# A four-direction selective scan: y kept in its direction's order, empty turns around DMAs, small operations moved from GpSimd to VectorE

## The chip, the cores and the metric

The kernel runs on one core of one Trainium2 chip. The metric is the device time of one execution in microseconds, the median of several runs. The engines are TensorE (PE, with PEld for its weight loads), VectorE (DVE), ScalarE (ACT), GpSimd (POOL) and SyncE (SP), which here issues all DMAs. Each takes its instructions in the order in which the program gives them, and waits at the first whose inputs are not ready.

## The reference, cut to what matters

The program is a sequence of four layers on x of shape (8, 64, 64, 64); the change touches the first one alone. There each image is normalised, projected to 128 channels of L = 4096 places, convolved (3 x 3, each channel by itself), scanned in four directions, normalised again, gated and projected back:

```python
xc = silu(_dwconv3(xc, conv_w, conv_b))
x_flat = xc.reshape(B, DI, L)                                   # row by row
x_t = jnp.transpose(xc, (0, 1, 3, 2)).reshape(B, DI, L)         # column by column
xs = jnp.concatenate([x_hwwh, jnp.flip(x_hwwh, axis=-1)], axis=1)
def step(h, inp):
    u_t, dt_t, B_t, C_t = inp
    h = h * jnp.exp(dt_t[..., None] * A) + dt_t[..., None] * B_t[:, :, None, :] * u_t[..., None]
    return (h, jnp.einsum('bkcn,bkn->bkc', h, C_t))
y = out_y[:, 0] + inv[:, 0] + wh + invwh                        # all put back in row order
y = _ln(y, outnorm_g, outnorm_b, LN_EPS) * jax.nn.silu(z)
return jnp.einsum('bhwd,cd->bhwc', y, outproj_w) + outproj_b
```

So a state of N = 16 numbers for each of 128 channels runs along L four times, and the four results are summed into y, place by place.

## The kernel before, in words

The 128 channels are the partitions. An image is 16 *steps*: four directions of four chunks of CH = 1024 places. A step has 16 *turns*, one for each n of the state. `steps` gives the order of directions: 0, 2, 1, 3 (rows forward, rows backward, columns forward, columns backward) and in the last image 1, 3, 0, 2, so that it ends in rows.

One turn (the loop at `for n in range(N)` and `unit`, L757 to 775):

- `z` is B_n of the chunk, spread over the partitions: by two matmuls from the bf16 pieces `bs` into PSUM (L737), or, for n in `BY_POOL` = (0, 3, 6, 8), by a product on GpSimd (L727) that ScalarE copies to PSUM (L734).
- ScalarE computes `a` = exp(dt A) (L719).
- VectorE multiplies `z` by dt u (L764; not for n in `BY_POOL`), then runs the scan `h` over 1024 places (L768).
- GpSimd multiplies `ct`, which a DMA has spread from DRAM (L715, 512 KB a turn, five buffers), by `h` (L773).
- TensorE sums `ct` into the chunk's PSUM tile `yps` (L810), two or three turns later (`sum_up`).

At turn 3 `begin_sum` opens the sum of the step: in an image's first direction from u (`skipd`), later from what y holds so far (L801). At turn 2 `empty` has had ScalarE copy the step before it out of PSUM into y (L783). The last chunk of a direction is the first of its reverse, so there the PSUM tile is kept and neither is needed. y lies in row order; for the column directions `ordered` reads and writes it with a stride of 64 elements.

Around that, `Background` holds a queue of *items*, each a pair (make, use): make's matmuls are issued in one turn, use's work on other engines in the next; `bg.later` puts a DMA another turn later. `(None, None)`, called `none`, is an empty turn. Turns in `idle` take an item only if it has no make. The items are the input norm, gates and convolutions of the next image, the projections of the next step (put first), and the output norm, gating and projection of the image before. `inverse_root` makes the two norms' chain: variances go to DRAM (`put`), come back spread over partitions (`fetch`), ScalarE takes the root, VectorE inverts, and the result goes to DRAM and comes back in rows (`back`), for a matmul that spreads it (`rps`, L393 and L445). In the last image the output norm is done two blocks at a time as they become ready, two items a turn.

The bf16 `pieces` of B (L667 to 700): one DMA brings `bw`, ScalarE rounds it to the first piece, GpSimd subtracts it (L681), ScalarE rounds the rest to the second (L684), GpSimd subtracts again for the third (L687), and DMAs store the three. `hooks` lays these, the step size's `soft` parts and `step_input` on turns 6 to 13 of each step. The gating product `z` times y is `multiply` (L566), on GpSimd, called from the norm's `apply` after the product of the next block.

Of the kernel before, what the change touches and what calls it, by code (L numbers as in the profile page):

```python
# [18 lines left out]
NB = 8  # L19
C = 64  # L20
S = 64
# [144 lines left out]
class Background:  # L166
# [7 lines left out]
    def __init__(self):  # L174
        self.queue, self.last, self.late = deque(), None, []
        self.groups, self.open, self.done = deque(), deque(), {}
        self.first = self.credit = 0
        self.item = False

    def add(self, items, first=False):  # L180
# [41 lines left out]
    def finish(self, b, count):  # L222

        while self.done.get(b, NBK) < count:
            self.credit = 1
            self.before(slots=NBK)
            self.after()

    def drain(self):
# [5 lines left out]
def scan_layer(cm, x_in, w, xh):  # L235

    tc, nc = cm.tc, cm.nc
    with ExitStack() as ctx:
# [90 lines left out]
        def inverse_root(nb):  # L329

            var = dr.tile([L], F32, name="vard", tag="vard")[: nb * BK]
            rs = dr.tile([L], F32, name="rsd", tag="rsd")[: nb * BK]
            sm = {}

            def put(ps, n, at):
                t = work.tile([NBK, BK], F32, name="vrow", tag="rstd", bufs=1)
                nc.scalar.copy(t[:n], ps[:n])
                bg.later(lambda: nc.sync.dma_start(
                    var[at * BK : (at + n) * BK].rearrange("(o n) -> o n", o=n), t[:n]
                ))  # L340
# [12 lines left out]

            def back(_):
                sm["r"] = work.tile([NBK, BK], F32, name="rstd", tag="rstd", bufs=1)[:nb]
                nc.sync.dma_start(sm["r"], rs.rearrange("(j f) -> j f", j=nb))

            chain = [none, (None, fetch), none, (None, root), (None, invert), none, (None, back), none]
            return put, chain, sm

        def norm_x(xn, pairs, project_in):

            put, chain, sm = inverse_root(2 * len(pairs))
            i0, sq = pairs[0], {}

            def centre(i):
                def make():
                    ps = bank("cps")
                    nc.tensor.matmul(ps, ln1_cen, xn[:, i, :], start=True, stop=True)
                    return ps  # L370

                def use(ps):
                    nc.scalar.copy(xn[:, i, :], ps)
# [12 lines left out]

            def apply(i):
                r = 2 * (i - i0)

                def make():  # L390
                    ps = bank("rps")
                    rows = ln1_row[: 2 * len(pairs), r : r + 2, :].rearrange("k e c -> k (e c)")
                    nc.tensor.matmul(ps, rows, sm["r"], start=True, stop=True)  # L393
                    return ps

                def use(ps):
                    x = xn[:, i, :]
                    nc.vector.tensor_tensor(x, x, ps, ALU.mult)
                    nc.scalar.activation(x, x, AF.Identity, bias=ln1_b, scale=ln1_g)

                return make, use

            out = [centre(i) for i in pairs[:2]] + [none] * (2 - len(pairs[:2]))
            for i in pairs:
                out.append(variance(i))
                if i + 2 in pairs:
                    out.append(centre(i + 2))
            out += chain
            out += [apply(i) for i in pairs[:2]] + [none] * (2 - len(pairs[:2]))
            for i in pairs:  # L410
                out += [project_in(2 * i), project_in(2 * i + 1)]
                if i + 2 in pairs:
                    out.insert(-1, apply(i + 2))
            return out

        def norm_y(y, blocks, load, multiply, project_out):
# [38 lines left out]
                return make, use  # L455

            out = [(None, lambda _: [square(j) for j in blocks[:2]]), none]
            out += [variance(j) for j in blocks] + chain
            out.insert(-2, (None, lambda _: [load(j) for j in blocks[:3]]))
            out += [apply(j) for j in blocks[:2]]  # L460
            end = (None, lambda _: multiply(blocks[-1]))
            if nb == 2:
# [1 line left out]
            for j in blocks:  # L464
                if j + 2 in blocks:
                    out.append(apply(j + 2))
                    if j + 2 == blocks[-1]:
                        out.append(end)
                out.append(project_out(j))
            return out  # L470


# [2 lines left out]
        def before(b):  # L475
# [70 lines left out]

            items = [[(None, load(j)) for j in range(NBK)]]
            for pairs in FIRST if b == 0 else (range(NBK // 2),):
                items.append(norm_x(xn, pairs, project_in))
            return u, zd, items, [gate(j) for j in range(NBK)], [convolve(j) for j in range(NBK)]  # L550

        def after(b, y, zd, blocks=range(NBK)):
# [10 lines left out]

            def multiply(j):
                z = gated[j][1]
                nc.gpsimd.tensor_tensor(z, z, y[:, bass.ts(j, BK)], ALU.mult)  # L566

            def project_out(j):
                def make():
# [97 lines left out]
        def pieces(ctl, low):  # L667
# [10 lines left out]

            def subtract():
                low["r"] = work.tile([128, 2, 128], F32, name="br", tag="br", bufs=1)  # L680
                nc.gpsimd.tensor_tensor(low["r"], low["b"], low["p"][:, 0], ALU.subtract)  # L681

            def second():
                nc.scalar.copy(low["p"][:, 1], low["r"])  # L684

            def third():
                nc.gpsimd.tensor_tensor(low["p"][:, 2], low["r"], low["p"][:, 1], ALU.subtract)  # L687

            def store():
                low["bsd"] = dr.tile([2, 3 * N, CH], BF16, name="bsd", tag="bsd", bufs=8)  # L690
# [85 lines left out]

        full = []

        def empty():

            if full:
                ctl = full.pop()
                nc.scalar.copy(  # L783
                    ordered(ctl["y"], ctl["k"], ctl["c"]),
                    ctl["ps"].rearrange("p (a b) -> p a b", b=S),
                )

        kept = []

        def begin_sum():  # L790
# [4 lines left out]
                ctl["ps"] = kept.pop()  # L795
                return
            ctl["ps"] = psy.tile([DI, CH], F32, name="yps", tag="yps")
            wt, src = (skipd, ctl["u"]) if ctl["new_y"] else (ctl["mat"], ctl["y"])
            so, half = ordered(src, ctl["k"], ctl["c"]), BK // S
            for i in range(CH // BK):  # L800
                nc.tensor.matmul(  # L801
                    ctl["ps"][:, bass.ts(i, BK)].rearrange("p (a b) -> p a b", b=S),
# [28 lines left out]
        def prepare(b, s):  # L831

            if b not in images:
                return None
            u, zd, y = images[b]
            k, c, i = steps(b)[s]
            bg.finish(b, 2 * c + 2 if s < NCH and k == 0 else NBK)
            low = lows.setdefault((b, k % 2, c), {}) if k < 2 else lows.pop((b, k % 2, c))
            dt, ut, e, items, soft = project(u, k, c, low)
            if b == 0 and s < NCH:  # L840
# [1 line left out]
            bg.add(items, first=True)  # L842
            new = work.tile([DI, N], F32, name="state", tag="state", bufs=3)
            ctl = dict(
                k=k, c=c, u=u, y=y, dt=dt, bc=low["bc"][k // 2], ut=ut, dus=e, soft=soft, new=new, state=None,
                first=(i == 0), new_y=(s < NCH), turns=(s % (2 * NCH) == NCH - 1),
                mat=lno_cen if s >= 3 * NCH - 1 else cm.ident,
            )
# [6 lines left out]

        def start(b):
            u, zd, items, gates, convs = before(b)
            y = io.tile([DI, L], F32, name="y", tag="y")
            images[b] = (u, zd, y)
            bg.add(items[0] + items[1])  # L860
            if b == 0:
                bg.add(convs[0] + convs[1])
# [9 lines left out]
        with tc.manual_schedule():  # L872
# [15 lines left out]
            for b in range(NB):  # L888
                for s in range(4 * NCH):
# [5 lines left out]
                    else:  # L895
                        nxt = prepare(b + 1, 0)
                    bg.credit = 2 if b == NB - 2 else 1
                    idle = () if early or late else (3, 6, 7, 8)
                    hooks = {}
                    if nxt:  # L900
                        do = nxt["pieces"]
# [4 lines left out]
                            }  # L906
                        else:
                            hooks = {14 - len(do) + i: [f] for i, f in enumerate(do)}
                            for i, f in zip((6, 7, 8), nxt["soft"]):
                                hooks[i] = hooks.get(i, []) + [f]  # L910
                            hooks[11] = hooks.get(11, []) + [lambda: step_input(nxt)]

                    def ahead(do, m, *args):
# [5 lines left out]
                    for n in range(N):  # L919
# [28 lines left out]
                            ahead(product, N)  # L948

                        if s == 0 and n == LAG + 2 and b > 0:  # L950
                            bg.add(after(b - 1, images[b - 1][2], images.pop(b - 1)[1]))
                        if late and n == LAG + 2:
                            c = 4 * NCH - s
                            bg.add(after(b, images[b][2], images[b][1], range(2 * c, 2 * c + 2)))
                        if s == (1 if b else NCH) and n == 0 and b + 1 < NB:
                            bg.add(later.pop(NCH, []))
                            start(b + 1)
# [5 lines left out]
            while pending:  # L963
                sum_up()
            empty()
            bg.add(after(NB - 1, images[NB - 1][2], images[NB - 1][1], range(2)))
            bg.drain()


# [1146 lines left out]
```

## Time and profile before

| | us |
|---|---|
| median of 3 runs (12468.33 to 12488.72) | 12470.36 |
| the profiled execution | 12474.25 |
| its span, first to last instruction | 12472.4 |
| scan layer, by the timeline, to about | 7200 |

The page's table of busy time over the whole span:

```profile
PE 11350.5 (91%) x38827; PEld 4100.1 (33%) x38827; DVE 10374.0 (83%) x7334; ACT 7820.0 (63%) x10296; POOL 7404.9 (59%) x3510
```

and its costliest groups inside the scan layer:

```profile
L773 POOL TENSOR_TENSOR ct<-ct,h 128x1024 f32<-128x1024 f32 x2048 | 4796.5, 2363 | 391.5 <-DMA ct<-bc 183.9
L768 DVE TENSOR_TENSOR_SCAN h<-a,state,z 128x1024 f32<-128x1024 f32 x1536 | 3572.4, 2342 | 96.0 <-ACT z L734 43.0
L764 DVE TENSOR_TENSOR z<-z,e 128x1024 f32<-128x1024 f32 x1536 | 1865.9, 1215 | 310.9 <-PE z L737 196.0
L727 POOL TENSOR_TENSOR bt<-bt,e 128x1024 f32<-128x1024 f32 x512 | 1210.8, 2365 | 4.5 <-DMA bt<-bc 4.5
```

A line has the source line, the engine, the operation, what it writes and reads with the shapes, the number of instructions; then the busy time and the mean duration in ns; then how long the engine stood idle just before these instructions, and what ended most of it. Busy shares over the whole span mix this layer with the later ones: in the scan layer GpSimd and VectorE are both nearly always at work.

### The profile page before, as it was taken

Reading aid. Unit: us, or ns where it says so; the run is one execution under the profiler, and the core shown is the slowest. Engines: PE = TensorE matmul, PEld = TensorE weight load, DVE = VectorE, ACT = ScalarE, POOL = GpSimd, SP = SyncE. Lnnn points to the kernel's source line nnn. Section 1 sums busy time; section 2 is a strip of 40 time slices with the busy share of each in tenths; the row PEclk is TensorE's granted clock in tenths of the full one; section 3 lists DMA queues with packets and bytes.
Section 4 is the critical chain, followed back from the end, with each engine's and each line's share of the span. In section 5 each row is a group of like instructions: output and inputs, shape, how many; then the busy total and the mean of one; then the engine's idle time right before and its main releaser. Section 6 shows DMA issues by size and latency. Waiting matters only on the chain. (4 is left out here: it accounts for less than half of the span.)

```text
span 12472.4 us, 119759 instructions
## 1 busy us (share of the span) xinstructions
PE 11350.5 (91%) x38827; PEld 4100.1 (33%) x38827; DVE 10374.0 (83%) x7334; ACT 7820.0 (63%) x10296; POOL 7404.9 (59%) x3510
## 2 busy tenths in 40 slices
PE   7899998999999999999998889999987778999999
PEld 2233332332333323323322232332334463333333
DVE  4999999999999999999989857768687785676767
ACT  4776766766766767767666545546456584555554
POOL 4999999999999999999999800000005490000000
PEclk8999999999999999999989889999998789999999
DMA  3666656656666666666566510000011100000000
GB/s 110 208 210 211 210 200 221 211 202 214 210 203 212 207 212 213 202 218 205 198 206 204 179 34 18 12 25 6 18 38 40 41 24 23 17 6 17 6 11 6
DMA packets 541331, 1562.17 MB, mean 125 GB/s; under 512 B 127360, under 2 KB 144400, under 8 KB 538128
## 3 DMA queue, kind: packets, MB, share of 16 engines
q1 hardware_dynamic: 540688, 1554.36, 37.8%
q8 instruction: 310, 5.08, 0.2%
q14 instruction: 333, 2.73, 0.1%
HBM read 1456.41 MB, written 88.87 MB: 124 GB/s over the span
## 5 line engine op out<-in xcount | busy, mean ns | idle before, releaser
L773 POOL TENSOR_TENSOR ct<-ct,h 128x1024 f32<-128x1024 f32 x2048 | 4796.5, 2363 | 391.5 <-DMA ct<-bc 183.9
L768 DVE TENSOR_TENSOR_SCAN h<-a,state,z 128x1024 f32<-128x1024 f32 x1536 | 3572.4, 2342 | 96.0 <-ACT z L734 43.0
L1117 DVE TENSOR_TENSOR sum<-sum,ex 128x1024 f32<-128x1024 f32 x1920 | 2347.5, 1223 | 617.9 <-ACT ex L1110 483.0
L1110 ACT ACTIVATE ex<-sc 128x1024 f32<-128x1024 f32 x2048 | 1968.0, 1024 | 1359.7 <-PE sc L1105 1359.3
L810 PE MATMUL yps<-ct,ident 128*128 128x512 f32 x5632 | 2810.5, 629 | 6.9 <-POOL ct L773 6.8
L719 ACT ACTIVATE a<-dt,amat 128x1024 f32<-128x1024 f32 x2048 | 2345.0, 1146 | 718.1 <-DVE h L768 711.7
L764 DVE TENSOR_TENSOR z<-z,e 128x1024 f32<-128x1024 f32 x1536 | 1865.9, 1215 | 310.9 <-PE z L737 196.0
L1124 PE MATMUL av<-ex,v 128*64 128x512 f32 x8192 | 1950.0, 604 | 0.0
L1105 PE MATMUL sc<-q,k 16*128 16x512 f32 (+1 forms) x8192 | 1562.2, 623 | 4.2 <-ACT q L1098 3.1
L810 PEld LDWEIGHTS yps<-ct,ident 128*128 128x128 f32 x5632 | 1009.0, 194 | 1390.9 <-issue 1253.2
L737 PE MATMUL z<-bs,pick 48*128 48x512 bf16 x3072 | 957.0, 393 | 447.0 <-DVE h L768 398.5
L810 PE MATMUL yps<-ct,lno_cen 128*128 128x512 f32 x2560 | 1313.1, 646 | 0.5 <-POOL ct L773 0.5
L768 DVE TENSOR_TENSOR_SCAN h<-a,z 128x1024 f32<-128x1024 f32 x512 | 1163.1, 2283 | 80.8 <-ACT z L734 51.2
L727 POOL TENSOR_TENSOR bt<-bt,e 128x1024 f32<-128x1024 f32 x512 | 1210.8, 2365 | 4.5 <-DMA bt<-bc 4.5
L1431 POOL TENSOR_TENSOR gt<-gt,pad 128x1024 f32<-128x1024 f32 x16 | 34.9, 2184 | 1571.1 <-ACT gt L1430 1492.5
L1124 PEld LDWEIGHTS av<-ex,v 128*64 128x64 f32 x8192 | 512.2, 136 | 1332.8 <-issue 1278.9
L734 ACT COPY z<-bt 128x1024 f32<-128x1024 f32 x512 | 519.7, 1015 | 589.0 <-POOL bt L727 316.4
L1105 PEld LDWEIGHTS sc<-q,k 16*128 16x128 f32 (+1 forms) x8192 | 528.4, 184 | 1016.1 <-issue 977.2
L737 PEld LDWEIGHTS <-pick 48*128 48x128 bf16 x3072 | 177.7, 95 | 1709.6 <-DVE h L768 888.0
L810 PEld LDWEIGHTS yps<-ct,lno_cen 128*128 128x128 f32 x2560 | 468.6, 198 | 637.3 <-issue 560.7
L530 PE MATMUL vps<-pad,convd 128*128 128x512 f32 x1152 | 545.9, 597 | 0.0
L1804 DVE RECIPROCAL r<-e 128x512 f32<-128x512 f32 x128 | 420.6, 3322 | 0.0
(416 smaller groups left out, 10539.4 us busy)
## 6 DMA issues: line engine op xcount, KB each, us to landing
ct<-bc SPq DMA_DIRECT2D x2048, 512.0 KB
bt<-bc SPq DMA_DIRECT2D x512, 512.0 KB
x<-x SPq DMA_DIRECT2D x12, 2048.0 KB
bc<-e SPq DMA_DIRECT2D x128, 128.0 KB
zd<-z SPq DMA_DIRECT2D x64, 256.0 KB
z<-zd SPq DMA_DIRECT2D x64, 256.0 KB
x<-x SPq DMA_DIRECT2D x32, 512.0 KB
part<-x SPq DMA_DIRECT2D x128, 128.0 KB
```

Source lines behind the costliest of these rows:

```text
L530: nc.tensor.matmul(held[0].rearrange("p (r c) -> p r c", c=S), convd[:, t, :], pad[:, j * rows + dy : (j + 1) * rows + dy, dx : dx + S], s ...
L719: ctl["exp", n] = nc.scalar.activation(ctl["a", n], ctl["dt"], AF.Exp, scale=amat[:, ctl["k"], n : n + 1])
L727: nc.gpsimd.tensor_tensor(bt, bt, ctl["dus"], ALU.mult)
L737: nc.tensor.matmul(z[:, bass.ts(i, BK)], pick[:, n : n + 1].to_broadcast([3 * N, DI]), ctl["bs"][:, bass.ts(i, BK)], start=True, stop=True,)
L764: first = nc.vector.tensor_tensor(z, z, ctl["dus"], ALU.mult)
L768: nc.vector.tensor_tensor_scan(h[:, flip], a[:, flip], z[:, flip], 0.0 if state is None else state[:, n : n + 1], ALU.mult, ALU.add,)
L773: freed[at] = nc.gpsimd.tensor_tensor(ct, ct, h, ALU.mult)
L810: nc.tensor.matmul(ctl["ps"][:, bass.ts(i, BK)], ctl["mat"], ct[:, bass.ts(i, BK)], start=False, stop=(n == N - 1 and not ctl["turns"]),)
L1105: nc.tensor.matmul(sc[:, e, :], k[r : r + d, bass.ts(j, 128)], qs[i][r : r + d, :], start=True, stop=True,)
L1110: nc.scalar.activation(ex, sc, AF.Exp)
L1117: nc.vector.tensor_tensor(sums[i], sums[i], ex, ALU.add)
L1124: nc.tensor.matmul(avs[i][r, :], v[:, j, r], ex[:, e, :], start=(j == 0), stop=(j == TQ - 1))
```

## The change

It has five parts.

1. y is two tiles an image, "row" and "col". `layout` allots each at its first use; the second takes the buffer that holds the image before's final y, so it calls `bg.flush(b - 1)`, which runs items until that image's output is done (an item adds b - 1 to `flushed`). `begin_sum` reads y always in its own direction's order. `empty` writes it in the order that the next reader needs (`into`), which at the end of a pair of directions is the other one, and copies in two halves of 512.
2. The chain of the norms has three more empty turns: one ahead of the root, two after `back`. There is one after each projection out, and, from the second image on, after each pair of projections in.
3. The output norm's first three loads of `xr` and `z` no longer stand as one item ahead of `back`, but one by one among the variances.
4. The fetch of `bw` moves from turn 7 to turn 6, `soft` parts go ahead of other work of their turn, and turn 3 is no longer in `idle`.
5. `multiply` and both subtractions of `pieces` are VectorE's instead of GpSimd's.

The diff, cut to its core:

```diff
+    def flush(self, b):
+        while b >= 0 and b not in self.flushed:
+            self.before()
+            self.after()
...
-            chain = [none, (None, fetch), none, (None, root), (None, invert), none, (None, back), none]
+            chain = [none, (None, fetch), none, none, (None, root), (None, invert), none]
+            chain += [(None, back), none, none, none]
...
                 out += [project_in(2 * i), project_in(2 * i + 1)]
                 if i + 2 in pairs:
                     out.insert(-1, apply(i + 2))
+                if b:
+                    out.append(none)
...
-            out += [variance(j) for j in blocks] + chain
-            out.insert(-2, (None, lambda _: [load(j) for j in blocks[:3]]))
+            for j in blocks:
+                out.append(variance(j))
+                if j in blocks[1:6:2] or nb == 2:
+                    at = j if nb == 2 else j0 + (j - j0) // 2
+                    out.append((None, lambda _, at=at: load(at)))
+            out += chain
...
-                out.append(project_out(j))
+                out += [project_out(j), none]
...
-                nc.gpsimd.tensor_tensor(z, z, y[:, bass.ts(j, BK)], ALU.mult)
+                nc.vector.tensor_tensor(z, z, y[:, bass.ts(j, BK)], ALU.mult)
...
-                nc.gpsimd.tensor_tensor(low["r"], low["b"], low["p"][:, 0], ALU.subtract)
+                nc.vector.tensor_tensor(low["r"], low["b"], low["p"][:, 0], ALU.subtract)
...
-                nc.gpsimd.tensor_tensor(low["p"][:, 2], low["r"], low["p"][:, 1], ALU.subtract)
+                nc.vector.tensor_tensor(low["p"][:, 2], low["r"], low["p"][:, 1], ALU.subtract)
...
+        def layout(b, name):
+            im = images[b]
+            if name not in im:
+                first = ("row", "col")[steps(b)[0][0] % 2]
+                if name != first:
+                    bg.flush(b - 1)
+                at = b % 2 if name == first else 1 - b % 2
+                im[name] = io.tile([DI, L], F32, name="y", tag=f"y{at}", bufs=1)
+            return im[name]
+
+        def own(t, c):
+            return t[:, bass.ts(c, CH)].rearrange("p (a b) -> p a b", b=S)
...
-                nc.scalar.copy(
-                    ordered(ctl["y"], ctl["k"], ctl["c"]),
-                    ctl["ps"].rearrange("p (a b) -> p a b", b=S),
-                )
+                mine = ("row", "col")[ctl["k"] % 2]
+                dst = layout(ctl["b"], ctl["into"])
+                out = own(dst, ctl["c"]) if ctl["into"] == mine else ordered(dst, 1, ctl["c"])
+                half = BK // S
+                for i in range(CH // BK):
+                    nc.scalar.copy(
+                        out[:, i * half : (i + 1) * half, :],
+                        ctl["ps"][:, bass.ts(i, BK)].rearrange("p (a b) -> p a b", b=S),
+                    )
...
-            wt, src = (skipd, ctl["u"]) if ctl["new_y"] else (ctl["mat"], ctl["y"])
-            so, half = ordered(src, ctl["k"], ctl["c"]), BK // S
+            half = BK // S
+            if ctl["new_y"]:
+                wt, so = skipd, ordered(ctl["u"], ctl["k"], ctl["c"])
+            else:
+                mine = ("row", "col")[ctl["k"] % 2]
+                wt, so = ctl["mat"], own(layout(ctl["b"], mine), ctl["c"])
...
+            ks = [steps(b)[q * NCH][0] % 2 for q in range(4)] + [0]
+            q = s // NCH
...
-                k=k, c=c, u=u, y=y, dt=dt, ...
+                b=b, k=k, c=c, u=u, into=("row", "col")[ks[q + q % 2]], dt=dt, ...
...
-                    idle = () if early or late else (3, 6, 7, 8)
+                    idle = () if early or late else (6, 7, 8)
...
                             hooks = {14 - len(do) + i: [f] for i, f in enumerate(do)}
+                            hooks[6] = hooks.pop(7, [])
                             for i, f in zip((6, 7, 8), nxt["soft"]):
-                                hooks[i] = hooks.get(i, []) + [f]
+                                hooks[i] = [f] + hooks.get(i, [])
...
                         if s == 0 and n == LAG + 2 and b > 0:
-                            bg.add(after(b - 1, images[b - 1][2], images.pop(b - 1)[1]))
+                            last = images.pop(b - 1)
+                            bg.add(after(b - 1, last["row"], last["zd"]))
+                            bg.add([(None, lambda _, b=b - 1: bg.flushed.add(b))])
```

More of the change, by code (lines that the diff above doesn't have):

```diff
@@ L177, in __init__ @@
         self.first = self.credit = 0
+        self.flushed = set()
         self.item = False
@@ L356, in back, with norm_x @@
                 nc.sync.dma_start(sm["r"], rs.rearrange("(j f) -> j f", j=nb))
-            chain = [none, (None, fetch), none, (None, root), (None, invert), none, (None, back), none]
+            chain = [none, (None, fetch), none, none, (None, root), (None, invert), none]
+            chain += [(None, back), none, none, none]
             return put, chain, sm
-        def norm_x(xn, pairs, project_in):
+        def norm_x(b, xn, pairs, project_in):
             put, chain, sm = inverse_root(2 * len(pairs))
@@ L548, in before @@
             for pairs in FIRST if b == 0 else (range(NBK // 2),):
-                items.append(norm_x(xn, pairs, project_in))
+                items.append(norm_x(b, xn, pairs, project_in))
             return u, zd, items, [gate(j) for j in range(NBK)], [convolve(j) for j in range(NBK)]
@@ L834, in prepare @@
                 return None
-            u, zd, y = images[b]
+            u = images[b]["u"]
             k, c, i = steps(b)[s]
+            ks = [steps(b)[q * NCH][0] % 2 for q in range(4)] + [0]
+            q = s // NCH
             bg.finish(b, 2 * c + 2 if s < NCH and k == 0 else NBK)
@@ L844, in prepare @@
             ctl = dict(
-                k=k, c=c, u=u, y=y, dt=dt, bc=low["bc"][k // 2], ut=ut, dus=e, soft=soft, new=new, state=None,
+                b=b, k=k, c=c, u=u, into=("row", "col")[ks[q + q % 2]], dt=dt, bc=low["bc"][k // 2], ut=ut, dus=e, soft=soft, new=new, state=None,
                 first=(i == 0), new_y=(s < NCH), turns=(s % (2 * NCH) == NCH - 1),
@@ L857, in start @@
             u, zd, items, gates, convs = before(b)
-            y = io.tile([DI, L], F32, name="y", tag="y")
-            images[b] = (u, zd, y)
+            images[b] = {"u": u, "zd": zd}
             bg.add(items[0] + items[1])
@@ L950, in scan_layer @@
                         if s == 0 and n == LAG + 2 and b > 0:
-                            bg.add(after(b - 1, images[b - 1][2], images.pop(b - 1)[1]))
+                            last = images.pop(b - 1)
+                            bg.add(after(b - 1, last["row"], last["zd"]))
+                            bg.add([(None, lambda _, b=b - 1: bg.flushed.add(b))])
                         if late and n == LAG + 2:
                             c = 4 * NCH - s
-                            bg.add(after(b, images[b][2], images[b][1], range(2 * c, 2 * c + 2)))
+                            bg.add(after(b, images[b]["row"], images[b]["zd"], range(2 * c, 2 * c + 2)))
                         if s == (1 if b else NCH) and n == 0 and b + 1 < NB:
@@ L965, in scan_layer @@
             empty()
-            bg.add(after(NB - 1, images[NB - 1][2], images[NB - 1][1], range(2)))
+            last = images[NB - 1]
+            bg.add(after(NB - 1, last["row"], last["zd"], range(2)))
             bg.drain()
```

## The prediction, before the changed kernel ran

> **What bounds the kernel now.** I read the page's busy table, then the answer by windows, then the groups and waits of VectorE and GpSimd in one long window of the scan layer, and last the lines that the diff touches. The change lies in the scan layer alone, whose scans run from about 93 to 7168 us.
>
> ```profile
> core 0: us, PE busy (x) PEld busy (x) DVE busy (x) ACT busy (x) POOL busy (x), PEclk, DMA share, GB/s
> 900.00:6300.00 5400.00, 5028.40 (x11322) 1695.90 (x11320) 5091.57 (x2866) 3809.84 (x5374) 5189.26 (x2333) 0.97 0.63 209
> ```
>
> In this window GpSimd is busy 96.1%, VectorE 94.3%. It holds 1589 scans, and an image has 256, so an image takes 5400 / 1589 x 256 = 870 us and the window holds 6.2 images. VectorE works 820 us of each and is idle 50; GpSimd works 836. Neither is alone the limit: every turn is a VectorE scan, then a GpSimd product on its result. What ends VectorE's 50 us stands in its waits:
>
> ```profile
> DVE z L764 <- PE z L737: 130.5, 125, 4.1
> DVE h L768 <- POOL ct L773: 25.1, 41, 1.1
> DVE y L450 <- PE rps L445: 21.3, 6, 4.7
> DVE z L764 <- POOL ct L773: 21.3, 25, 1.6
> DVE z L764 <- ACT dt L633: 18.3, 13, 3.0
> ```
>
> TensorE's `z` is the largest part, 130.5 / 6.2 = 21 us an image, GpSimd 46.4 / 6.2 = 7.5 us. Two reasons for TensorE's lateness are visible. First, matmuls that take y in the other direction's order:
>
> ```profile
> L801 PE MATMUL yps<-y,ident x144: 592/1034/1222, 1316.7 to 5941.3; 128*128 128x512 f32 x144
> L801 PE MATMUL yps<-y,lno_cen x104: 1033/1035/1107, 935.1 to 6215.5; 128*128 128x512 f32 x104
> L801 PE MATMUL yps<-u,skipd x100: 592/592/1105, 1044.1 to 6270.9; 128*128 128x512 f32 x100
> ```
>
> The middle figure is the median: 1034 ns strided, 592 in order. Second, a wait that holds TensorE's queue, once an image in the output norm:
>
> ```profile
> 2010.31 2.04 PE L445 MATMUL rps<-rstd,ident 8*128 8x512 f32 x2 [5.96 <-DMA rstd<-rsd]
> 2012.28 1.03 PE L737 MATMUL z<-bs,pick 48*128 48x512 bf16 x2
> ```
>
> TensorE stands 5.96 us; the `z` behind it is late too. SyncE's timeline shows why: the read back of `rsd` went out at 2004.19, behind six loads of `xr` and `z` issued at one go from 1998.23.
>
> [...] No VectorE instruction in this scan loop has two SBUF tensors (`z` and `rps` are in PSUM), so the trace doesn't show this pair. It shows the neighbouring case, a VectorE operation of one input beside GpSimd's memsets:
>
> ```profile
> L117 DVE TENSOR_SCALAR p_cen<-ident x2: 948/1012/1076, 7205.1 to 7206.2; 64x64 f32<-64x64 f32 x2
> L304 DVE TENSOR_SCALAR ln_cen<-ident x2: 180/186/191, 5.1 to 5.3; 64x64 f32<-64x64 f32 x2
> ```
>
> The same shape took 186 ns away from the memsets and 1012 beside them[...].
>
> **The change part by part**, per image.
>
> *y in its direction's order.* Before, the third and fourth quarters read y strided: 3 + 4 begins of 4 matmuls, 28 x 0.442 = 12.4 us of TensorE; afterwards none does. ScalarE still writes strided in two quarters (8 emptyings, before 7), each now in two halves; L783 takes 1.00 us in order and 1.91 strided, so two halves cost some 0.2 more, 14 x 0.2 = 3 us. ScalarE is busy 71% in the window; this is hidden unless a begin waits for it. Of the 19 us of `z` waits left when the norm's share is off (2 us, below) I take 14 as gone: the turn after the begin and, in the same steps, the `z` three turns on. Bounds: 7 to 19. The tile shared between images needs the old image's norm done by the fifth step of the next: 49 items, against 11 + 4 x 16 turns less about 16 taken by projections, so no stop there.
>
> *Empty turns.* The output norm's chain gains three empty turns and its loads go out in three pairs among the variances, six DMAs off SyncE's queue just ahead of `rsd`. The 5.96 us wait needs two turns of 3.4 us, so it goes: VectorE gets back 21.3 / 6 = 3.5 us at L450 and some 2 us of `z` behind it, 5 us. The input norm's chain and the empty turns between projections hold no engine; the queue of items grows from some 177 to 198 in 16 steps of 12 (now 13) turns for TensorE's items, 208 places, so it still fits, but the gates and convolutions come about two steps later. In the last image, items run two a turn and the same waits return in each of three steps. From 6988 to 7167 us VectorE waits 13.6 us for `rps` and 12.9 for ScalarE's root. The three turns behind the read back are one and a half there, 5 us, which covers the first (longest single wait 5.4); the one turn more ahead of the root is half a turn, 1.7 us in each of three: 13 + 5 = 18 us, once.
>
> *Off GpSimd.* 8 x 1.277 us of products and 16 x 0.675 of subtractions: 21 us of 836. Of VectorE's 7.5 us behind GpSimd I take 6. ScalarE's wait for the first subtraction (251.4 us in all, 63 times) falls with it, but ScalarE has room: 2 us. The fetch of `bw` moves one turn earlier, past one `ct` load on SyncE (0.3 us of issue). SyncE's wait for L687 before the store of the pieces, which holds `ct` loads behind it, becomes a wait for VectorE, over by then.
>
> *Onto VectorE.* [...] Then the wait for the ports, W, for each of 24. Behind a waiting instruction stand the next turn's product and scan, and GpSimd, ScalarE and TensorE behind these. W is nothing where GpSimd has caught up and itself waits for the scan, since VectorE's next instruction is there first; it is half of GpSimd's 2.363 us, 1.2, where GpSimd is always in the middle of one. GpSimd will have more room than before, but a product behind the norm's 0.66 us operation meets a `ct` just begun. I take 0.4, so 9.6 us.
>
> Sum: -14 - 5 - 6 - 2 + 12.2 + 9.6 = -5 us an image. The first image, with its own stalls, I leave out (its early steps do both subtractions in one turn, so VectorE waits there for ScalarE's cast between them: 0 to 5 us in each of three, kept for the range). 7 x 5 + 18 = 53 us less. The profiled execution took 12474.25 us, 1.85 more than its span, and lies 3.9 above the median of the runs shown: 12474 - 53 = 12421, said as 12420.
>
> **The rivals.**
>
> *More gain.* No contention worth the name (W = 0) and most of the `z` waits gone (19 in place of 14): -5 - 9.6 - 5 = -20 an image; 7 x 20 + 18 = 158 less, about 12315. For it: GpSimd loses 2.5% of its work[...]. Against it: GpSimd was reading SBUF 96% of the time.
>
> *Slower: the ports decide.* Each of the 24 instructions waits for the rest of a GpSimd instruction, W = 1.2: 28.8 us in place of 9.6, so +14 an image; 7 x 14 - 18 = +80, about 12555. It decides from W = (14 + 5 + 6 + 2 - 12.2) / 24 = 0.6 us on. For it: L117 above waited nearly all of a memset. Against: VectorE's delay gives GpSimd time to catch up, which shortens the next wait.
>
> *The crowd moves.* The gates (two loads of ScalarE's table each) now fall into the steps that prepare the column direction, with their lower projections and copies of `ut`; in the step where they lie now (2282 to 2339 us) ScalarE is busy 49.1 of 57 us and VectorE idle 3.6. If that comes up in each of two steps instead[...] it eats the 5 us: about 12470.
>
> That flush stops everything is a rival too, but the count above leaves it no room.
>
> **How the numbers follow.** Forecast 0.42, more gain 0.22, slower 0.26, the moved crowd 0.10. No change means within 0.2%, 25 us, about what a measurement can tell. The forecast's own range is 12370 to 12470 (W from 0.1 to 0.7), faster in eight of ten of it. Faster: 0.42 x 0.8 + 0.22 + 0.10 x 0.3 + 0.01 = 0.60. Within: 0.42 x 0.15 + 0.10 x 0.4 + 0.26 x 0.1 = 0.13. Slower: the rest, 0.27. The range over all cases: 12295 to 12555.
>
> **What would show it.** The L801 rows at 592 ns on y throughout; no `rps` wait for `rstd` over 1 us in the norm; GpSimd's 192 small operations gone, and its busy share down by two points. On VectorE the product's mean duration says W outright: about 1.1 us as forecast, 0.7 for more gain, 1.9 for slower; the subtractions 0.8, 0.4 and 1.6. I am wrong if the product takes its bare time and the span still doesn't fall, if TensorE's `z` waits stay at 20 us an image with L801 in order, or if a stretch of turns appears in which items run at one go.

## The result, and the profile after

| | before | changed |
|---|---|---|
| median, us | 12470.36 (12460.50 to 12488.72, 5 runs) | 12530.37 (12517.99 to 12532.37, 5 runs) |
| profiled execution, us | 12474.25 | 12519.95 |
| its span, us | 12472.4 | 12518.1 |

The ratio is 1.0043, with a 95% interval of 1.0028 to 1.0057: slower by 0.43%. The forecast, 12420 us and faster, was wrong. The time lies outside the forecast's own range (12370 to 12470), inside the range over all cases (12295 to 12555), and 25 us below the rival "the ports decide" (12555). The profiled execution lost 45.7 us, and the scan layer accounts for nearly all of it: its last scan ends at 7210 us, 43 later than before.

Below, an *image mean* is the time from an image's first scan to the next image's, averaged over the second to the sixth image of one trace. It was 868.1 us before and is 880.7 now. The first image is 10 us shorter than before and the last 28 (929.0 against 939.4, 886.2 against 914.0), so the loss is in the ones between.

First, the answer by windows for the changed kernel, in the long window that the prediction used (columns as there):

```profile
900.00:6300.00 5400.00, 4964.65 (x11181) 1686.76 (x11180) 5194.49 (x2967) 3770.32 (x5383) 5025.45 (x2153) 0.95 0.63 206
```

VectorE went from 5091.57 to 5194.49 us busy, although the window now holds fewer scans; GpSimd fell from 5189.26 to 5025.45, three points. Scaled to an image mean, VectorE's busy time rose from 94.3% of 868.1 to 96.2% of 880.7 us: 819 to 847. Its idle time fell from 50 to 33. What VectorE gained in fewer waits it lost to longer work.

The groups of VectorE in that window name the work (count, then busy time and mean duration in ns):

```profile
L580 DVE TENSOR_TENSOR z<-z,y 128x512 f32<-128x512 f32 x48 | 98.1, 2043 | 0.0
L695 DVE TENSOR_TENSOR br<-bw,bp 128x256 f32<-128x256 f32 x48 | 78.3, 1632 | 5.6 <-ACT bp L691 5.3
L460 DVE TENSOR_TENSOR y<-y,rps 128x512 f32<-128x512 f32 x48 | 31.8, 662 | 3.6 <-PE rps L455 3.6
L701 DVE TENSOR_TENSOR bp<-br,bp 128x256 bf16<-128x256 f32 x48 | 31.0, 646 | 0.0
```

L460 and L580 are the same operation on the same shape, but L460 reads one operand from PSUM. It takes 0.66 us, the product 2.04. The wait for GpSimd is no idle time in this view; it lies inside the instruction's own duration. The shortest product took 0.658 us and the shortest subtractions 0.396 and 0.398.

What still makes VectorE idle, from the answer on its waits (total, times, longest):

```profile
DVE z L778 <- PE z L751: 80.2, 78, 4.5
DVE h L782 <- ACT z L748: 41.3, 21, 4.1
DVE z L778 <- POOL ct L787: 11.5, 16, 1.8
...
DVE y L460 <- PE rps L455: 3.6, 3, 1.3
DVE h L782 <- POOL ct L787: 1.6, 3, 0.7
```

TensorE's `z` fell from 130.5 to 80.2, `rps` from 21.3 to 3.6, GpSimd's two lines from 46.4 to 13.1. All that was to go did go, in part or whole. One wait grew, which the prediction did not have: the scan's wait for the `z` that ScalarE copies, from 14.5 to 41.3, some 4 us an image. The begins that read y are in order (shortest, median, longest in ns):

```profile
L839 PE MATMUL yps<-y,ident x192: 592/592/1221, 441.5 to 6891.6; 128*128 128x512 f32 x192
```

The opposite side shows in GpSimd's waits, of before and then of the changed kernel:

```profile
POOL ct L773 <- DMA ct<-bc: 136.8, 114, 4.4
POOL ct L773 <- DVE h L768: 35.9, 31, 3.6
```

```profile
POOL ct L787 <- DVE h L782: 209.6, 180, 4.6
POOL ct L787 <- DMA ct<-bc: 99.3, 101, 5.3
```

Before, GpSimd waited mostly for its loads. Now it waits mostly for VectorE's scan, six times as long as before: VectorE has become the later of the two.

How one such wait looks, in the timeline of the changed kernel (start, length), VectorE and then GpSimd:

```profile
2093.96 0.66 DVE L460 TENSOR_TENSOR y<-y,rps 128x512 f32<-128x512 f32 x1
2094.54 2.63 DVE L580 TENSOR_TENSOR z<-z,y 128x512 f32<-128x512 f32 x1
2097.09 2.33 DVE L782 TENSOR_TENSOR_SCAN h<-a,state,z 128x1024 f32<-128x1024 f32 x1
```

```profile
2094.27 2.35 POOL L741 TENSOR_TENSOR bt<-bt,e 128x1024 f32<-128x1024 f32 x1
2096.59 2.80 POOL L787 TENSOR_TENSOR ct<-ct,h 128x1024 f32<-128x1024 f32 x1
```

GpSimd began `bt` at 2094.27, VectorE its product 0.27 us later. The product ended at 2097.17, 0.55 us after `bt`. GpSimd's next instruction, begun meanwhile, took 2.80 us, where the median `ct` of this trace takes 2.36.

The whole trace shows the same. Of its 64 products, 59 began while GpSimd was at work, and each of these ended 0.55 to 0.58 us after a GpSimd instruction did. The other five found GpSimd idle and took 0.67 to 0.69 us.

### The profile page after: what moved, and what is told of

Its sections match the earlier page's. It is cut to its first block, busy times and chain, and to the rows that moved or that the text cites. A ratio compares the mean times of both kernels' runs of the same rounds, so it can differ in the third digit from the quotient of the medians.

```text
span 12518.1 us, 120237 instructions
## 1 busy us (share of the span) xinstructions
PE 11316.7 (90%) x38827; PEld 4104.1 (33%) x38827; DVE 10606.6 (85%) x7526; ACT 7829.3 (63%) x10409; POOL 7285.3 (58%) x3318
## 5 line engine op out<-in xcount | busy, mean ns | idle before, releaser
L848 PE MATMUL yps<-ct,ident 128*128 128x512 f32 x5632 | 2880.1, 643 | 0.0
L848 PE MATMUL yps<-ct,lno_cen 128*128 128x512 f32 x2560 | 1287.7, 635 | 1.6 <-POOL ct L787 1.6
```

What stands on the lines that cost most here:

```text
L848: nc.tensor.matmul(ctl["ps"][:, bass.ts(i, BK)], ctl["mat"], ct[:, bass.ts(i, BK)], start=False, stop=(n == N - 1 and not ctl["turns"]),)
```

## The experiments

Each was timed beside the kernel before, and what is said of times rests on the ratios to it. The figures by image come from one profiled execution of each kernel. In the edits, `gpsimd` and `vector` are the two engines' forms of the same instruction. "The ports" in the expectations is a name for the wait of VectorE's products and subtractions behind GpSimd: the traces show the wait, and that it lasts to the end of a GpSimd instruction (0.55 to 0.58 us before the product's own end), not what makes it.

**The fifth part alone, on the kernel before.** Two edits of engine in `pieces` and one in `multiply`:

```diff
-                nc.gpsimd.tensor_tensor(z, z, y[:, bass.ts(j, BK)], ALU.mult)
+                nc.vector.tensor_tensor(z, z, y[:, bass.ts(j, BK)], ALU.mult)
```

> The kernel before with part 5 alone: the gating product and both subtractions on VectorE, all else as before. Theory of the ports (a VectorE instruction with two SBUF inputs waits until GpSimd's instruction in progress ends): the product takes 1.9 to 2.5 us in the mean instead of its bare 0.69, the first subtraction 1.3 to 1.8 instead of 0.40; VectorE is busy some 25 to 32 us an image more, and the kernel is slower than before by 80 to 200 us (12550 to 12670). Rival, the moved crowd (parts 1 to 4 put gates and convolutions into worse steps and that is what cost the time): part 5 alone is within 40 us of before, or faster by up to 60 because GpSimd loses 21 us an image.

12562.39 us, ratio 1.0083 (1.0067 to 1.0099). The part is a loss without the others too. The mean of the first subtraction is 1.49 us on VectorE, that of the second a bare 0.395, and the product's group reads

```profile
L566 DVE TENSOR_TENSOR z<-z,y 128x512 f32<-128x512 f32 x48 | 99.1, 2064 | 0.0
```

**The fifth part undone in the changed kernel** (the same lines, the other way).

> The changed kernel with part 5 undone: product and subtractions on GpSimd again, parts 1 to 4 as changed. Theory of the ports: parts 1 to 4 keep their gain, VectorE's idle time falls by 10 to 18 us an image, and the kernel is faster than before by 70 to 150 us (12320 to 12400), so 130 to 210 below the changed kernel. Rival, the moved crowd: it stays within 40 us of the changed kernel's 12530, above before.

12313.64 us (12305.36 to 12318.17), ratio 0.9883 (0.9869 to 0.9898). This beats both kernels, so parts 1 to 4 are worth 1.2%, and the fifth takes 1.6% away. The window, in the columns of above:

```profile
900.00:6300.00 5400.00, 5016.19 (x11494) 1712.51 (x11493) 5156.81 (x2908) 3879.09 (x5556) 5264.84 (x2369) 0.97 0.63 212
```

GpSimd is busy 97.5% here, and the kernel is still the fastest. The clock granted to TensorE is 0.97 where the changed kernel had 0.95, but VectorE's waits for TensorE's `z` don't show it: they are 84.9 us here and 80.2 there.

**The product alone undone, and the subtractions alone undone.** One line of the edit each.

> The changed kernel with the gating product alone back on GpSimd. Theory of the ports: VectorE loses 8 instructions an image of 2.04 us in the mean, 16 us, and GpSimd gains 10; the time falls by 60 to 110 us from the changed kernel, to 12420 to 12470. Rival, the moved crowd: within 30 us of the changed kernel.

> The changed kernel with the two subtractions alone back on GpSimd. Theory of the ports: VectorE loses 8 x 1.63 and 8 x 0.65 us an image, 18 us, GpSimd gains 11; the time falls by 40 to 110 us, to 12420 to 12490. The second subtraction took its bare 0.40 us in most steps, so nearly all of it is the first. Rival, the moved crowd: within 30 us of the changed kernel.

12438.54 us, ratio 0.9983 (0.9974 to 0.9993), with the product back on GpSimd, and 12425.28 us, 0.9973 (0.9964 to 0.9982), with the subtractions back. So against the kernel with all of them on GpSimd, the subtractions alone cost 1.0% of the time before and the product alone 0.9%: neither part carries the loss by itself. The group that remains on VectorE is no shorter: the product's mean is 2.49 us in the second kernel, and in the first the subtractions have

```profile
L695 DVE TENSOR_TENSOR br<-bw,bp 128x256 f32<-128x256 f32 x50 | 93.2, 1864 | 5.5 <-ACT bp L691 5.3
...
L701 DVE TENSOR_TENSOR bp<-br,bp 128x256 bf16<-128x256 f32 x49 | 31.4, 641 | 0.0
```

**The product with one operand in PSUM.** ScalarE writes the normalised y into the PSUM buffer of `rps`, which the norm has just read, and the product on VectorE takes it from there. Number, shape and place of the products stay; what goes is their second SBUF input.

```diff
-                    nc.scalar.activation(v, v, AF.Identity, bias=on_b, scale=on_g)
+                    nc.scalar.activation(ps, v, AF.Identity, bias=on_b, scale=on_g)
+                    held[j] = ps
...
-                nc.vector.tensor_tensor(z, z, y[:, bass.ts(j, BK)], ALU.mult)
+                nc.vector.tensor_tensor(z, z, ps, ALU.mult)
```

> The changed kernel, but ScalarE writes the normalised y of a block into the PSUM bank of its rps instead of back into SBUF, and VectorE's gating product takes it from there: as many VectorE instructions of the same size, one SBUF input instead of two. Theory of the ports: the product falls from 2.04 us in the mean to its bare 0.66 to 0.70, VectorE loses 11 us an image, and the time falls by 60 to 120 us from the changed kernel (12530) to some 12410 to 12470, like the kernel with the product on GpSimd (12439). Rival, plain work (it is the added instruction in VectorE's queue and what stands behind it that costs, not the second SBUF input): the product may get shorter, but the time stays within 30 us of the changed kernel.

12454.0 us, ratio 0.9992 (0.9983 to 1.0), 0.51% less than the changed kernel. The product is at its bare time, in the same place:

```profile
L581 DVE TENSOR_TENSOR z<-z,rps 128x512 f32<-128x512 f32 x48 | 32.5, 677 | 0.0
```

It lost 1.37 us each, eight an image, 10.9 us; the image mean fell by 10.3 (880.7 to 870.4). Of these products too, 58 of 64 began while GpSimd was at work, and the longest took 0.69 us. So the product's extra length, 2.04 us against 0.68, was a wait that in these runs went with its second SBUF operand, and in the image mean it cost nearly its full length; the whole time fell by some 64 us, where eight images would make 87.

**The same with the subtractions on GpSimd.**

> As the one before (product on VectorE with y from PSUM), with both subtractions back on GpSimd. Theory of the ports: no VectorE instruction of the scan loop has two SBUF inputs any more; the product costs VectorE 5.5 us an image and spares GpSimd 10; near the kernel with part 5 undone (12314), 12270 to 12350. Rival, plain work: the product on VectorE costs as in the changed kernel, 12400 to 12450.

12333.81 us, ratio 0.9892 (0.9877 to 0.9907), 0.09% above the kernel with all of them on GpSimd, which is inside the two intervals. The product's bare 5.4 us an image on VectorE and 10.2 us less on GpSimd all but cancel; whether the first was hidden or the second paid for it isn't told apart. Taking work off GpSimd won nothing that can be seen.

**The first part alone** (y in its direction's order, the rest as before).

> Part 1 alone: y in its direction's order, chains, loads, hooks and engines as before. By the prediction 14 us of z waits an image go, some 100 us: 12340 to 12390. Rival, the norm's wait is the larger part of the gain of parts 1 to 4 (143 us) and the waits for z were only partly due to strided reads: 12400 to 12440.

12368.27 us, ratio 0.9919 (0.9905 to 0.9932). The image mean fell from 868.1 to 860.4. From VectorE's waits:

```profile
DVE z L771 <- PE z L744: 78.2, 71, 3.9
...
DVE y L457 <- PE rps L452: 18.9, 6, 4.0
```

`z` from TensorE is already where the changed kernel has it; `rps` is not. The whole time fell by some 101 us, where the prediction's 14 us in seven images make 98.

**The first and fourth parts** (from the kernel with the fifth undone, the chains and loads of before put back).

```diff
-            chain = [none, (None, fetch), none, none, (None, root), (None, invert), none]
-            chain += [(None, back), none, none, none]
+            chain = [none, (None, fetch), none, (None, root), (None, invert), none, (None, back), none]
...
-                out += [project_out(j), none]
+                out.append(project_out(j))
```

> Parts 1 and 4: as part 1 alone, with the earlier fetch, the soft parts first and turn 3 open to items; no empty turns, and the three loads in one item ahead of the read back. By the prediction within 15 us of part 1 alone, and the empty turns with the spread loads are worth 53 us: the kernel with part 5 undone (12314) should lie 35 to 70 below this one. Rival: the empty turns are worth nothing on the whole because the gates come later: within 20 us of 12314.

12367.42 us, ratio 0.9924 (0.9911 to 0.9938): the fourth part does nothing that shows in the time. But the wait for `rps` in the long window is nearly gone here, without an empty turn:

```profile
DVE y L457 <- PE rps L452: 2.2, 1, 2.2
```

So in the middle images, by these two traces, it was the fourth part that took it away, and that alone gained nothing in the time. The second and third together are the step from here to 0.9883, 0.4%; which of the two it is was not tried. By images, from this trace to that of the fifth part undone: the last 882.4 to 865.2, the first 931.9 to 920.8, the mean 855.6 to 853.4. The last figure is unsure by more than its size: the profiled execution here lies 13 us below its median, and the image mean 4.8 us below that of part 1 alone, at equal medians.

**The product ahead of the norm's operation** (subtractions on GpSimd; compare with the kernel that has those alone undone).

```diff
+                    if j - 1 in blocks:
+                        multiply(j - 1)
...
-                    if j - 1 in blocks:
-                        multiply(j - 1)
```

> The kernel is the changed one with the subtractions back on GpSimd and the gating product issued ahead of the norm product in the same step, so that it no longer stands right behind the 0.66 us norm product. Theory (the phase decides: behind the norm product the gating product meets a ct that has just begun, and waits for all of it): the mean of the product falls from 2.49 us to 0.8 to 1.4 us, and the time comes to 12325 to 12395 us. Rival (VectorE waits as long wherever the product stands, because GpSimd runs ct almost without a gap): the mean stays above 1.7 us and the time within 25 us of 12425.

12400.7 us, ratio 0.9951 (0.9937 to 0.9964), against 0.9973. Over the whole trace (shortest, median, longest in ns):

```profile
L580 DVE TENSOR_TENSOR z<-z,y x64: 658/950/7258, 1169.7 to 7095.7; 128x512 f32<-128x512 f32 x64
```

The median fell from 2.55 to 0.95 us, the mean in the window only from 2.49 to 1.59, above the 1.4 expected; the time gained 0.2%, with intervals that touch, lies 6 us above the range expected, and is just inside what the rival allowed. The median supports the phase theory: counted one by one in the traces, 37 of 64 products met a GpSimd instruction that had begun less than 0.7 us earlier, and 13 of 64 here; the time, taken alone, decides nothing. Standing right behind a scan (59 of 64 now do) the product found GpSimd idle only 11 times; 30 times it met an instruction more than 1.8 us old and waited for its short rest. A few very long waits keep the mean up, the three longest at the same turn of three images. GpSimd's timeline at the longest:

```profile
4598.94 6.95 POOL L787 TENSOR_TENSOR ct<-ct,h 128x1024 f32<-128x1024 f32 x3
4605.85 2.33 POOL L741 TENSOR_TENSOR bt<-bt,e 128x1024 f32<-128x1024 f32 x1
```

The product began at 4601.48, when GpSimd was in the second of the three `ct`, and ended at 4608.74: GpSimd's next two instructions went ahead of it as well, after which GpSimd stood idle for 3.54 us.

**The softplus addition two turns later** (product of the gate on GpSimd; compare with the kernel that has that alone undone). The third `soft` part, which is the addition L659 on GpSimd (a neighbour in GpSimd's queue, not in VectorE's), moves from turn 8 to turn 10, from ahead of the first subtraction to ahead of the second.

```diff
-                            for i, f in zip((6, 7, 8), nxt["soft"]):
+                            for i, f in zip((6, 7, 10), nxt["soft"]):
```

> The kernel is the changed one with the gating product back on GpSimd and the softplus piece that stands ahead of the first subtraction moved from turn 8 to turn 10, so that the first subtraction has another neighbour on VectorE. Theory (what stands right ahead on VectorE sets the wait): the mean of the first subtraction falls from 1.86 us to 0.4 to 1.0 us, and that of the second rises from 0.64 us to 1.2 to 2.4 us; the time stays within 40 us of 12439. Rival (the neighbour does not matter): both means stay within 0.3 us of 1.86 and 0.64 us.

12490.11 us, ratio 1.0024 (1.0014 to 1.0033), against 0.9983.

```profile
L701 DVE TENSOR_TENSOR bp<-br,bp 128x256 bf16<-128x256 f32 x49 | 83.7, 1709 | 0.0
L695 DVE TENSOR_TENSOR br<-bw,bp 128x256 f32<-128x256 f32 x49 | 72.7, 1484 | 5.5 <-ACT bp L691 5.4
```

The second subtraction rose from 0.64 to 1.71 us, as the theory had it: without the move GpSimd stood idle at the start of 44 of the 64, here of none. The first fell only to 1.48, not below 1.0, and the time rose by 52 us, more than the 40 allowed. So what GpSimd is given just ahead sets the wait of the second; the first meets a GpSimd instruction in progress either way (57 times in 64 here, 63 without the move).

## Why the prediction was wrong

Set against what VectorE was given, the traces line up. The middle column is the mean durations in the window times their number (8 products, 8 of each subtraction an image):

| kernel with parts 1 to 4 and | VectorE's added time an image | image mean |
|---|---|---|
| all three on GpSimd | 0 | 853.4 |
| product from PSUM | 5.4 | 854.1 |
| product, ahead of the norm's | 12.7 | 858.9 |
| product | 19.9 | 868.4 |
| subtractions | 20.0 | 870.4 |
| subtractions, product from PSUM | 23.9 | 870.4 |
| subtractions, softplus later | 25.5 | 875.8 |
| all three (the change) | 34.6 | 880.7 |

Some 3 to 7 us of it don't show in the image; the rest lengthens it, whichever instruction it comes from. What hides the 3 to 7 us, idle time of VectorE or the work taken off GpSimd, isn't told apart. Each row is one execution; the third ran 29 us below its kernel's median, some 4 us an image, the others within 13 us of theirs.

*The step that failed* is W, the wait of each of the 24 instructions behind GpSimd. The prediction expected the wait, wrote that "a product behind the norm's 0.66 us operation meets a `ct` just begun", and then took 0.4 us, against the 1.2 of a GpSimd that is always busy (half of 2.363), because GpSimd "will have more room than before". No trace that it had showed a VectorE instruction with two SBUF operands beside a GpSimd instruction, so that there would be a wait was assumed and the 0.4 was a guess. Nor did a trace show the bare work on VectorE, 12.2 us an image in its sum; the bare times measured since, 0.68 us (the product from PSUM) and 0.40 us (the subtractions that found GpSimd idle), make 8 x 0.68 + 16 x 0.40 = 11.8. Over 0.69 us, the longest of the five products that found GpSimd idle, and 0.40 the runs have 1.35 us for the product, 1.23 for the first subtraction, 0.25 for the second: 8 x 2.83 = 22.6 us an image in place of 9.6. The 13 us are the whole miss of the fifth part: forecast at -6 - 2 + 12.2 + 9.6 = +13.8 an image, measured at 880.7 - 853.4 = +27.3. They are also nearly the whole miss of the forecast: the other four parts came to 1.17%, 146 us, where its terms make 7 x 19 + 18 = 151; the fifth came to some 200 where they make 7 x 13.8 = 97. The average, 0.94 us, lies above the 0.6 from which, by the prediction's own sum, the kernel gets slower.

Why more room on GpSimd didn't help: GpSimd did catch up, as its waits for `h` show, but there it begins `ct` soon after the scan: 0.23 us after its end, in the median of the 242 waits for `h` in the changed kernel's trace. Of the 50 products and subtractions that found GpSimd idle there, 48 stood directly behind a scan. The gating product stood second, behind L460, in 53 cases of 64, and in the changed kernel's trace met an instruction less than 0.7 us old 35 times in 64: 13 times after such a catching up, 22 times after GpSimd had gone straight on, as in the timeline above. Why the two engines run in step in these 22 wasn't tried. The second subtraction found GpSimd idle 44 times in 64, and then took its bare 0.40 us. The first found GpSimd idle once in 64, though it stood right behind a scan in 63. It fell in the turn after the softplus addition, an extra GpSimd instruction (2.42 us in the mean), but with that moved away it still found GpSimd idle only 7 times; why GpSimd is late there stays open. That the wait lasts to the end of a GpSimd instruction is seen at both operations: 59 products ended 0.55 to 0.58 us after one, and 60 of the first subtractions 0.28 to 0.29 us.

*y in its direction's order.* The begins took 592 ns, as forecast. ScalarE's two halves together took 0.16 us more than the whole copy in order and 0.21 more strided (medians 585 and 1067 ns a half, 1007 and 1926 before), near the 0.2 forecast. The `z` waits fell from 130.5 / 6.2 = 21 to 78.2 / 6.3 = 12 us an image, 9 in place of 14, and the image mean of this part alone fell by 7.7: the mechanism right, its size in the middle images over-stated, inside the bounds of 7 to 19. That the whole time still fell by the 98 us of the sum is partly luck: of the 93 us that the scan layer lost in this trace, 39 lie in the five images of the mean, and 55 in the first, the seventh and the last. The image mean with parts 1 to 4 fell by 868.1 - 853.4 = 14.7 where I had 19.

*Empty turns.* The `rps` wait of the middle images went as forecast, but for another reason: the fourth part, added to the first, takes it away, and the time doesn't fall with it. So the 5 us an image forecast for the empty turns aren't shown; by the traces the middle images gained 2.2 us, with the doubt named above, and the longer wait for ScalarE's `z` (40.4 us with the fifth part undone, 15.1 with part 1 alone) stands against it. The last image's 18 us came true at 17.2. VectorE's waits there, before, between 6988 and 7167 us:

```profile
DVE y L450 <- PE rps L445: 13.6, 4, 5.4
DVE vsm L351 <- ACT vsm L348: 12.9, 3, 5.5
```

and changed, between 6950 and 7200, also within the last image's scans, where neither is left and this is the largest:

```profile
DVE z L778 <- PE z L751: 5.2, 7, 1.7
```

In the last 179 us of scans with parts 1 and 4 alone they still stand at 9.7 and 12.6 us, so here it is the empty turns or the spread loads that remove them. The first image, which I left out, gained another 11 in that pair of traces. The sum of 53 us for these parts thus came true (0.4%, some 51 us), but in good part by luck, with the first image in place of the middle ones.

*Off GpSimd, 6 + 2 us.* VectorE's waits behind GpSimd did fall, but the kernel in which GpSimd loses its products and VectorE pays only their bare time gains nothing that shows: the 5.4 us of bare products and the 10.2 us off GpSimd cancel. The busiest GpSimd of the study, 97.5%, belongs to the fastest kernel.

*The sum.* I added the parts, but they do not add. The fifth costs 0.83% on the kernel before, with 50 us of idle VectorE an image, and 1.60% on top of the other four, with 38 (4.5% of 853.4). So the four parts, worth 1.17% alone, are worth 0.40% beside it. That the fifth part's 0.83% alone, some 103 us, is close to the 97 of the prediction's terms is luck: W was twice its size there too (19.7 us an image in place of 9.6), but of the 31.6 us that VectorE was given, only 18.1 show in the image mean (886.2). That it is VectorE's idle time which hides the rest is argued from these figures, not tried.

*The rivals.* "The ports decide" was right in sign, and in that the instructions wait for the rest of a GpSimd instruction, as 59 of the 64 products did. "More gain" fell with the product's 2.04 us. "The crowd moves" fell with the kernel that keeps every moved turn and undoes the fifth part: 1.2% faster than before. What that rival foresaw did happen: in its trace ScalarE is busy 50.5 and 51.3 us in an image's eleventh and twelfth steps, against 42.9 and 42.0 before. But VectorE's idle time in these steps is 0.7 and 4.2 us, against 2.7 and 4.2 before. ScalarE's table loads, which that rival counts, took 1.28 us each in both kernels' traces.

## What to carry to other kernels

Before moving a small operation to an engine with some idle time, ask where its operands lie and what the other engine is doing at that very place in the turn. The shares of busy time didn't tell it here (GpSimd at 97.5% in the fastest kernel, 93.1% in the changed one), and the bare duration was only the lower end: 0.66 us for the shortest product, 2.04 in the mean. Giving the product one operand in PSUM took the wait away: 0.68 us. Putting it directly behind the scan, for whose result the other engine waits, let only 11 of 64 products find it idle, and gained 0.2% of the time. Judge the parts of a mixed change apart: here parts worth 1.2% hid inside a slower kernel.

## What the runs showed that was not expected

VectorE's turn doesn't always come after one GpSimd instruction. In the changed kernel the first subtraction outlasted more than one in 4 of 64 cases, for instance, VectorE first:

```profile
2388.81 5.81 DVE L695 TENSOR_TENSOR br<-bw,bp 128x256 f32<-128x256 f32 x1
```

```profile
2382.72 7.01 POOL L787 TENSOR_TENSOR ct<-ct,h 128x1024 f32<-128x1024 f32 x3
2389.65 2.40 POOL L659 TENSOR_TENSOR dt<-dt,e 128x1024 f32<-128x1024 f32 x1
2391.96 2.38 POOL L787 TENSOR_TENSOR ct<-ct,h 128x1024 f32<-128x1024 f32 x1
```

A 0.40 us subtraction waited for the last of three `ct`, for L659 and for another `ct`, 5.81 us. In the usual case, 59 of 64 for this subtraction and for the product, VectorE's instruction ended before GpSimd's next one did. That one was itself longer behind a waiting product, as the 2.80 us above: that is also the median of the 46 that began so, against 2.36 of all `ct`. What tells the two cases apart stays open; no run tried it.
